# Features between two layers dealt out anew, and A12·B21 of the weight product in inner form

## The chip, the cores and the metric

The kernel runs on one core of a Trainium2 chip. The metric is the device time of one execution in microseconds; the time before is the median of three runs. Engines: TensorE (PE, with its weight loads PEld), VectorE (DVE), ScalarE (ACT), GpSimd (POOL), and SyncE (SP), which here only issues transfers.

## The reference

Two residual layers with low-rank adapters, all in float32, x of 8 × 256 × 1024:

```python
# layer 0: idx0 picks one of 5 adapters per batch row
y = x + x @ W0.T + ((x @ A0[idx0]) @ B0.T) * 0.5          # A0: (5, 1024, 32), B0: (1024, 32)
# layer 1: idx1 picks one of 32 adapters per batch row
out = y + y @ W1.T + b1 + ((y @ A1[idx1]) @ B1[idx1]) * 2  # A1: (32, 1024, 16), B1: (32, 16, 1024)
```

W0 and W1 are 1024 × 1024.

## The kernel before, in words

The kernel first multiplies the two weights, M = (I + W0)ᵀ(I + W1)ᵀ, and then applies M to all eight batch rows, together with the adapters, folded into a few narrow products. The weight product is a 2 × 2 block product in the Strassen–Winograd form: seven products of 512 × 512 blocks, called P1 = A11·B11, P2 = A12·B21 and so on, and sums of blocks on VectorE. The A blocks lie in `w0n` (W0 as loaded, with the identity added), the B blocks in `w1T` (W1 transposed, with the identity added). Later products have the same form at two levels: each product of 512 is itself seven products of 256 (`product`, with `Operand` holding the four sums t1 to t4 of the right side and `z_sums` making the four sums of the left side; `form` puts the seven results together).

The contraction index of M is the 1024 features between the layers: rows of W0 and columns of W1. Each feature stands at a partition p (0 to 127) of one of eight chunks k; chunks 0 to 3 make A11 and B11, chunks 4 to 7 make A12 and B21. Before, feature 512·i + 4·p + m stands in chunk k = 4i + m at partition p.

The stage around the change, at the start of the kernel:

- SP issues the loads in program order: the first 256 rows of the first half of W1's rows (`load_w1`, L170, four transfers, one for each group of 32 partitions), the first column halves of chunks 0 to 3 of W0 (`load_w0`, L178), the other 256 rows, the second column half of these W1 rows, chunks 4 to 7 of W0's first column half, the second half of W1's rows (eight transfers), b0, and at last the second column half of all W0 chunks. Each row piece of W1 is 128 floats, 512 bytes.
- A transfer from SP or ACT uses one of eight semaphores in turn, and waits until the previous transfer of that semaphore has landed. Transfers of ACT and SP share them.
- VectorE transposes W1 chunk by chunk (`turn_w1`, L225) and adds the identity to chunks (L233, L185); part of the identity is added on POOL.
- TensorE computes P1 in half width as the transposes arrive (L951), ACT copies the four results to `m22` (`keep_p1`, L300), and then P2 is accumulated on top of P1 in the same four banks, four tiles of 128 rows with four matmuls of 512 columns each (`product2`, L286), and copied to `m11` (L310).
- ACT issues the eight gathers of a1, the layer 1 adapter rows, one for each batch row (`load_a1`, L198), between its copies; POOL copies each into place (L202).
- Then TensorE runs `prepare_down(0)` (L701, reads a1 and the first half of w0n), `prepare_up` (L676), `finish_up` (L690), `prepare_down(1)` (L701, reads the second half), `prepare_cross` (L715), and `product6` of the first tile (L286).

The order of the instructions on each engine is the order of the program text (a manual schedule); each engine works in order. The waits are put in by the framework. It finds that an instruction reads what another has written by the range of addresses of its operand within each partition.

Of the kernel before, what the change touches and what calls it, by code (L numbers as in the profile page):

```python
# [10 lines left out]
ALU = mybir.AluOpType  # L11
# [9 lines left out]
P = 128  # L21
NH = 512
# [5 lines left out]
NWARM = 15  # L28
NV7 = 7
# [5 lines left out]
NQ = NH // 2  # L35
NB = 4
NX = 2
SQ = 32
# [4 lines left out]
def kernel(  # L43
# [11 lines left out]
    lora_b1: bass.AP,  # L55
    out: bass.AP,
):

# [70 lines left out]
    def fix_indices(rawi, n: int, layer: int):  # L131
        wrap = const.tile([1, B], I32, tag=f"wrap{layer}", name=f"wrap{layer}")
        nc.vector.tensor_scalar(wrap, rawi, 0, n, ALU.is_lt, ALU.mult)
        fixed = const.tile([1, B], I32, tag=f"fixed{layer}", name=f"fixed{layer}")
        nc.vector.tensor_tensor(fixed, rawi, wrap, ALU.add)
        nc.vector.tensor_scalar(fixed, fixed, 0, n - 1, ALU.max, ALU.min)
        return fixed

    def index(fixed, b: int, n: int, engine=SP):
        return nc.values_load(  # L140
            fixed[0:1, b : b + 1],
            engines=[engine],
            min_val=0,
            max_val=n - 1,
            skip_runtime_bounds_check_because="clamped on the chip",
        )
# [11 lines left out]
                )  # L158
        return xq

    def new_w1(h: int, i: int):
        both = units[:, 4 * h + 2 * i : 4 * h + 2 * i + 2].rearrange("p u n -> p (u n)")
        return both.rearrange("p (t c) -> p t c", t=NR)

    def load_w1(wq, h: int, i: int, lo: int = 0, hi: int = NR):

        rows = slice(h * NH + lo * SQ, h * NH + hi * SQ)
        for g in range(NG):
            cols = slice(i * NH + g * P, i * NH + (g + 1) * P)
            nc.sync.dma_start(  # L170
                wq[g * SQ : (g + 1) * SQ, lo:hi, :],
                w1[rows, cols].rearrange("(t q) c -> q t c", q=SQ),
            )

    def load_w0(k: int, i: int):
        cols = slice(i * NH, (i + 1) * NH)
        rows = w0[(k // NB) * NH : (k // NB + 1) * NH, cols]
        nc.sync.dma_start(  # L178
            w0n[:, k, cols], rows.rearrange("(p m) c -> p m c", m=NB)[:, k % NB, :]
        )  # L180

    def diag_w0(k: int):
        diag = w0n[:, k].rearrange("p (i q m) -> p i m q", i=2, m=NB)[:, k // NB, k % NB]
        engine = nc.vector if k < NB else nc.gpsimd
        engine.tensor_tensor(diag, diag, ident, ALU.add)  # L185

    def load_b0():
        nc.sync.dma_start(
            b0.rearrange("p (i m) r -> p i (m r)", i=2),
            lora_b0.rearrange("(i p m) r -> p i (m r)", i=2, m=NB),  # L190
        )


    a1_rows = work[:, 0 : 2 * NH].rearrange("p (b k r) -> p b k r", b=B, k=NK)

    def load_a1(b: int):
        j = index(fixed1, b, N1, mybir.EngineType.Activation)
        nc.scalar.dma_start(  # L198
            a1_rows[:, b].rearrange("p (i m) r -> p i (m r)", m=NB),
            lora_a1[bass.ds(j, 1)].rearrange("o (i p m) r -> p (o i) (m r)", i=2, m=NB),  # L200
        )
        nc.gpsimd.tensor_copy(a1[:, :, b, :], a1_rows[:, b])  # L202

    def load_down(b: int):
# [15 lines left out]
            )  # L220


    def turn_w1(wq, h: int, k: int, lo: int = 0, hi: int = NR):
        cols = slice(h * NH + lo * SQ, h * NH + hi * SQ)
        nc.vector.transpose(  # L225
            w1T[:, k, cols].rearrange("p (t q) -> p t q", q=SQ),
            wq[:, lo:hi].rearrange("p t (q m) -> p m t q", m=NB)[:, k % NB],
        )
        if k // NB == h:
            part = slice(lo * SQ // NB, hi * SQ // NB)  # L230
            diag = w1T[part, k, cols].rearrange("p (q m) -> p m q", m=NB)[:, k % NB]
            engine = nc.vector if h == 0 else nc.gpsimd
            engine.tensor_tensor(diag, diag, ident[part, part], ALU.add)  # L233

    def turn_x(xq, unit: int):
        xT = units[:, unit].rearrange("p (k t) -> p k t", k=NB)
# [238 lines left out]
    def quarters(x):  # L475
        return x[:, 0:2, 0:P], x[:, 2:4, 0:P], x[:, 0:2, P:T], x[:, 2:4, P:T]

    def z_sums(x, z):
        x11, x12, x21, x22 = x
        nc.vector.tensor_tensor(z[0], x21, x22, ALU.add)  # L480
        nc.vector.tensor_tensor(z[1], z[0], x11, ALU.subtract)
        nc.vector.tensor_tensor(z[2], x11, x21, ALU.subtract)
        nc.vector.tensor_tensor(z[3], x12, z[1], ALU.subtract)


    SLOT = {2: 0, 3: 1, 4: 2, 5: 3, 7: 4, 1: 5, 6: 6}
# [3 lines left out]
    def slot(ps, i: int):  # L490
        n, pos = BANK[i]
        return ps[n][:, pos * NQ : (pos + 1) * NQ]
# [78 lines left out]
    def form(v, ps=None, dst=None):  # L571
# [21 lines left out]
        nc.vector.tensor_tensor(mid, src_two(3, 0), two(1), ALU.add)  # L593
        nc.vector.tensor_tensor(d[:, 3 * NQ : 4 * NQ], src(5), at(6), ALU.add)  # L594

    m12 = {}

    def sums_m(m: int):
# [5 lines left out]
    class Chain:  # L604
# [33 lines left out]
            z_sums(self.q(name), self.z[name])  # L638

        def preload(self):  # L640

            p = m22[:, self.tiles, :].rearrange("p m (h n) -> p (m h) n", h=2)
            for i, part in ((2, 0), (4, 2), (5, 3)):
                nc.scalar.copy(slot(self.X, i), p[:, part])
            nc.vector.tensor_tensor(slot(self.X, 3), p[:, 1], p[:, 3], ALU.subtract)
            for i in (1, 7):
                nc.vector.memset(slot(self.X, i), 0.0)

        def product(self, ps, name, which, first, low=None):
            product(ps, self.q(name), self.z[name], w_ops[which], first, low=low)  # L650
# [17 lines left out]
    def prepare_up():  # L668
        tile = work[:, 4 * NH : 6 * NH]
        part = [tile[:, h * NH : (h + 1) * NH] for h in range(NO)]  # L670
        for h in range(NO):
            cols = slice(h * NH, (h + 1) * NH)
            pm = new_bank()
            for k in range(NK):
                g = k % 4
                nc.tensor.matmul(  # L676
                    pm[g * R0 : (g + 1) * R0, :],
                    b0[:, k, :],
                    w1T[:, k, cols],
                    start=(k < 4),  # L680
                    stop=(k >= NK - 4),
                )
            nc.scalar.copy(part[h], pm)
        return part
# [13 lines left out]
    def prepare_down(h: int):  # L698
        pm = new_bank()
        for k in range(NK):  # L700
            nc.tensor.matmul(  # L701
                pm,
                a1[:, k].rearrange("p b r -> p (b r)"),
                w0n[:, k, h * NH : (h + 1) * NH],
                start=(k == 0),
                stop=(k == NK - 1),
            )
        nc.scalar.copy(gT[h], pm)
# [185 lines left out]
    with tc.manual_schedule(engines=ORDERED):  # L894
        make_identity(nc, ident)
        mid = NR // 2
        wq = {}
        wq[0, 0] = new_w1(0, 0)
        for n in range(2):
            load_w1(wq[0, 0], 0, 0, n * mid, (n + 1) * mid)  # L900
            if n == 0:
                for k in range(NB):
                    load_w0(k, 0)
        wq[0, 1] = new_w1(0, 1)
        load_w1(wq[0, 1], 0, 1)
        for k in range(NB, NK):
            load_w0(k, 0)
        for i in range(2):
            wq[1, i] = new_w1(1, i)
            load_w1(wq[1, i], 1, i)  # L910
        load_b0()
        for k in range(NK):
            load_w0(k, 1)
        nc.scalar.copy(s_all[:, 0:R0], ident[:, 0:R0])

        pw = banks[6][:, 0:P]
        for _ in range(NWARM):
            nc.tensor.matmul(pw, ident, ident, start=True, stop=True)
        raw0, raw1 = load_indices(idx0, 0), load_indices(idx1, 1)
        nc.gpsimd.memset(scale, L1_SCALING)  # L920
        for half in range(2):
# [27 lines left out]
        def first(g, k: int, n: int):  # L949
            cols = slice(n * NH // 2, (n + 1) * NH // 2)  # L950
            nc.tensor.matmul(  # L951
                g.p1[:, cols],
                g.a[0][:, k, :],
                w1T[:, k, cols],
                start=False,
                stop=(k == NB - 1),
                skip_group_check=True,
            )

        for k in range(NB):  # L960
            turn_w1(wq[0, 0], 0, k, 0, mid)
            diag_w0(k)
            for g in w_groups:
                first(g, k, 0)
        for k in range(NB):
            turn_w1(wq[0, 0], 0, k, mid, NR)
        for m, g in enumerate(w_groups):
            for k in range(NB):
                first(g, k, 1)
            g.keep_p1(m22[:, m, :])  # L970
        fixed0, fixed1 = fix_indices(raw0, N0, 0), fix_indices(raw1, N1, 1)
        for k in range(NB, NK):
            turn_w1(wq[0, 1], 0, k)
        for m, g in enumerate(w_groups):
            for b in range(3 * m, min(3 * m + 3, B)):
                load_a1(b)
            g.product2(m11[:, m, :])
        for k in range(NB):
            turn_w1(wq[1, 0], 1, k)
        for k in range(NB):  # L980
            turn_w1(wq[1, 1], 1, NB + k)
        for k in range(NB, NK):
            diag_w0(k)
        for k in range(NB):
            sums_w1_first(k)
        prepare_down(0)
        part = prepare_up()
        w_groups[0].sums()
        sums_w1_last()
        finish_up(part)  # L990
        prepare_down(1)
        prepare_cross()
        for which in ("t2", "t1"):
            w_ops[which].sums_dma()
# [286 lines left out]
```

## Time and profile before

| what | value |
|---|---|
| median of 3 runs | 336.01 us (335.77 to 336.64) |
| profiled execution | 336.54 us |
| its span, first to last instruction | 334.8 us |
| granted TensorE clock, mean | 0.999 |
| PE busy | 329.6 us, 98% of the span |
| DVE busy | 246.2 us, 74% |
| POOL busy | 67.9 us, 20% |
| ACT busy | 61.3 us, 18% |
| bytes moved by DMA | 34.53 MB |

Times in the profile count from the start of the span. A matmul in float32 stands as two records, so "x32" on a matmul line is 16 matmuls. A name such as `bank<-w1T,w0n` says which tile is written and which are read; L286 is line 286 of the kernel. In a line of the timeline the numbers are the start, the time that the group took, the engine, and in brackets the idle time of the engine before it and what ended it. "SPq" and "ACTq" are the issuing of transfers on these engines, and "issue" is time in which the engine waited for nothing that the profile shows. The chain that ended last is followed back from the last instruction, each time to what released it.

### The profile page before, as it was taken

How to read it: one execution, taken by the hardware profiler on the slowest of the kernel's cores; microseconds unless marked ns; L12 is line 12 of the kernel's file. 1: busy time of each engine (PE TensorE's matmuls, PEld its weight loads, DVE VectorE, ACT ScalarE, POOL GpSimd, SP SyncE). 2: the span in 40 equal slices, each digit the busy share in tenths (PEclk: the TensorE clock that was granted, in tenths of full speed). 3: DMA queues.
4: the chain of work that ended last, by engine and by line, in shares of the span. 5: the costliest groups of instructions: out<-in, count | busy, mean ns of one | idle time of the engine just before them, and what ended most of it. 6: DMA issues, size and time to landing. Idle time of an engine off the chain costs nothing.

```text
span 334.8 us, 4443 instructions
## 1 busy us (share of the span) xinstructions
PE 329.6 (98%) x1496; PEld 245.1 (73%) x1496; DVE 246.2 (74%) x466; ACT 61.3 (18%) x128; POOL 67.9 (20%) x125
## 2 busy tenths in 40 slices
PE   8999999999999999999999999999999999999996
PEld 8774434544488877888877887877888777788875
DVE  5752697159899999999997856985675986323964
ACT  1022043300034132440001330001331001322000
POOL 7001261540042232771023100012200010000000
PEclk9999999999999999999999999999999999999999
DMA  7949982990062980786277300275500121100113
GB/s 211 199 133 186 271 191 46 168 173 14 0 95 63 194 137 14 113 133 104 95 191 204 79 2 0 74 222 148 116 10 0 63 96 63 64 2 0 63 65 126
DMA packets 66399, 34.53 MB, mean 103 GB/s; under 512 B 47300, under 2 KB 61124, under 8 KB 66376
## 3 DMA queue, kind: packets, MB, share of 16 engines
q1 hardware_dynamic: 56520, 21.13, 27.9%
q0 software_dynamic: 7680, 12.59, 17.4%
q10 hardware_dynamic: 2176, 0.52, 1.0%
q8 instruction: 12, 0.20, 0.2%
q14 instruction: 11, 0.09, 0.1%
HBM read 19.55 MB, written 8.39 MB: 83 GB/s over the span
## 4 chain that ended last, share of the span: by engine, by line
PE 94%; DMA 2%; SPq 1%; DVE 1%; issue 0%; ACT 0%; DVEq 0%
PE bank L523 66%; PE bank L286 14%; PE bank L747 4%; PE bank L701 4%; DMA units<-in_L_cond_W_dram 2%; PE bank L951 2%; PE bank L676 1%; PE bank L765 1%; SPq L170 1%; DVE w1T L225 1%; PE bank L690 1%; SPq L178 1%; DVE w1T L233 0%; PE bank L736 0%; PE bank L715 0%
## 5 line engine op out<-in xcount | busy, mean ns | idle before, releaser
L509 DVE TENSOR_TENSOR work<-bank,work 128x512 f32<-128x512 f32 (+1 forms) x56 | 32.7, 620 | 19.0 <-PE bank L523 18.8
L505 ACT COPY work<-bank 128x512 f32<-128x512 f32 (+1 forms) x56 | 25.8, 548 | 43.0 <-PE bank L523 42.6
L225 DVE STREAM_TRANSPOSE w1T<-units 128x512 f32<-128x512 f32 (+1 forms) x20 | 17.3, 901 | 18.0 <-DMA units<-in_L_cond_W_dram 17.9
L888 POOL DMA_DIRECT2D out_dram<-work x12 | 9.0, 752 | 100.6 <-DVE work L594 100.6
L523 PE MATMUL bank<-w0n,w1T 128*128 128x256 f32 x104 | 24.6, 384 | 0.0
L755 ACT ACTIVATE a<-bank,shift,scale 128x256 f32<-128x256 f32 x8 | 4.5, 564 | 103.3 <-PE bank L747 103.3
L523 PEld LDWEIGHTS bank<-w0n,w1T 128*128 128x128 f32 x104 | 19.3, 190 | 4.1 <-issue 1.7
L523 PE MATMUL bank<-w0n,m 128*128 128x256 f32 x88 | 21.2, 384 | 0.0
L523 PE MATMUL bank<-w1T,s_all 128*128 128x256 f32 x80 | 20.2, 379 | 0.0
L238 DVE STREAM_TRANSPOSE units<-units 128x512 f32<-128x512 f32 x32 | 19.9, 676 | 0.2
L523 PEld LDWEIGHTS bank<-w0n,m 128*128 128x128 f32 x88 | 16.4, 190 | 3.4 <-issue 1.4
L523 PE MATMUL bank<-tw,m 128*128 128x256 f32 x68 | 17.5, 382 | 0.0
L523 PEld LDWEIGHTS bank<-w1T,s_all 128*128 128x128 f32 x80 | 15.2, 190 | 2.1
L523 PE MATMUL bank<-tw,s_all 128*128 128x256 f32 x64 | 16.1, 379 | 0.0
L747 PE MATMUL bank<-units,down 128*64 128x256 f32 x128 | 15.6, 385 | 0.0
L523 PE MATMUL bank<-m,units 128*128 128x256 f32 x64 | 15.1, 379 | 0.0
L951 PE MATMUL bank<-w1T,w0n 128*128 128x256 f32 x64 | 14.5, 383 | 0.5 <-DVE w1T L233 0.5
L523 PEld LDWEIGHTS bank<-tw,m 128*128 128x128 f32 x68 | 12.8, 190 | 2.4 <-issue 0.7
L523 PE MATMUL bank<-w0n,s_all 128*128 128x256 f32 x56 | 14.4, 379 | 0.0
L286 PE MATMUL bank<-tw,s_all 128*128 128x512 f32 x32 | 14.3, 595 | 0.0
L951 PEld LDWEIGHTS bank<-w1T,w0n 128*128 128x128 f32 x64 | 12.3, 196 | 2.4 <-DVE w1T L233 1.3
L701 PE MATMUL bank<-w0n,a 128*128 128x512 f32 x32 | 14.1, 592 | 0.0
(249 smaller groups left out, 646.8 us busy)
## 6 DMA issues: line engine op xcount, KB each, us to landing
units<-in_x_dram SPq DMA_DIRECT2D x128, 64.0 KB, 2.4
out_dram<-work POOLq DMA_DIRECT2D x12, 512.0 KB, 3.5
w0n<-in_L_cond_W_dram SPq DMA_DIRECT2D x16, 256.0 KB, 6.1
units<-in_L_cond_W_dram SPq DMA_DIRECT2D x12, 256.0 KB, 4.9
out_dram<-work SPq DMA_DIRECT2D x3, 512.0 KB, 3.2
units<-in_L_cond_W_dram SPq DMA_DIRECT2D x8, 128.0 KB, 4.6
down<-in_L_cond_lora_A_dram SPq DMA_DIRECT2D x32, 32.0 KB, 2.4
up<-in_L_cond_lora_Bs_dram SPq DMA_DIRECT2D x16, 64.0 KB, 2.7
```

The costliest lines, as they stand in the source:

```text
L170: nc.sync.dma_start(wq[g * SQ : (g + 1) * SQ, lo:hi, :], w1[rows, cols].rearrange("(t q) c -> q t c", q=SQ),)
L225: nc.vector.transpose(w1T[:, k, cols].rearrange("p (t q) -> p t q", q=SQ), wq[:, lo:hi].rearrange("p t (q m) -> p m t q", m=NB)[:, k % NB],)
L238: nc.vector.transpose(xT[:, NX * j : NX * (j + 1), :].rearrange("p c (t q) -> p c t q", q=SQ), xq[:, :, j, :].rearrange("p t (q c) -> p c ...
L286: nc.tensor.matmul(pm, a[:, k, :], b(k), start=first and k == 0, stop=(k == NB - 1), skip_group_check=not first,)
L505: nc.scalar.copy(at_home(v, n), whole(ps, n))
L509: nc.vector.tensor_tensor(at_home(v, n), whole(ps, n), at_home(v, n), ALU.add)
L523: nc.tensor.matmul(slot(ps, i) if dst is None else dst, lhs, rhs, start=BANK[i][0] not in started, stop=stop, skip_group_check=True,)
L701: nc.tensor.matmul(pm, a1[:, k].rearrange("p b r -> p (b r)"), w0n[:, k, h * NH : (h + 1) * NH], start=(k == 0), stop=(k == NK - 1),)
L747: nc.tensor.matmul(pl[half * MLOW : (half + 1) * MLOW, :], down[:, half * NB + k, :], x_b[half][:, k, :], start=(k == 0), stop=(k == NB - ...
L755: nc.scalar.activation(lows[:, b % NLOW], pl, mybir.ActivationFunctionType.Identity, bias=shift[:, 0:1], scale=scale[:, 0:1],)
L888: eng.dma_start(out[b, :, h * NH : (h + 1) * NH].rearrange("(j p) d -> p j d", p=P), ob[:, 0:D].rearrange("p (j d) -> p j d", d=NH),)
L951: nc.tensor.matmul(g.p1[:, cols], g.a[0][:, k, :], w1T[:, k, cols], start=False, stop=(k == NB - 1), skip_group_check=True,)
```

## The change

Feature 256·g + 128·i + 4·q + m now stands in chunk k = 4i + m at partition 32·g + q. So a group of 32 partitions holds 256 neighbouring columns of W1, both halves i, and one transfer of the second half of W1's rows reads row pieces of 256 floats, 1024 bytes. The first half of the rows is still loaded in pieces of 128 floats (`first`, `last`). W0, b0 and a1 are loaded in the same new order; b0 takes two transfers, and each a1 gather becomes two, the first half on ACT and the second on POOL. The diagonal on which the identity stands now lies apart for each group of partitions: `add_identity` does four chunks in one instruction, `add_identity_to` one chunk; all of them run on VectorE.

P2 = A12·B21 is computed in the inner form, for two tiles of 128 rows at a time (class `Second`): seven products of 256 columns with 256 features each, two matmuls a product, on banks that are loaded with parts of P1 beforehand (`load_inner`, `load_inner_3`, `zero_inner`), so that `form` gives P1 + P2 in `m11`. `prepare_down(1)` moves from behind `finish_up` to behind the identities, ahead of `prepare_up`, and the loads of W0's second column half move behind the identities of chunks 4 to 7 in the program. The warm-up matmuls write to four banks instead of one.

```diff
-    def load_w1(wq, h: int, i: int, lo: int = 0, hi: int = NR):
+    def load_w1(h: int, lo: int, hi: int, first: int = 0, last: int = 2):

         rows = slice(h * NH + lo * SQ, h * NH + hi * SQ)
         for g in range(NG):
-            cols = slice(i * NH + g * P, i * NH + (g + 1) * P)
+            cols = slice((2 * g + first) * P, (2 * g + last) * P)
             nc.sync.dma_start(
-                wq[g * SQ : (g + 1) * SQ, lo:hi, :],
+                wq[h][g * SQ : (g + 1) * SQ, lo:hi, first * P : last * P],
                 w1[rows, cols].rearrange("(t q) c -> q t c", q=SQ),
             )
...
+    def add_identity(t, i: int, first: int, last: int):
+
+        part = slice(first * SQ, last * SQ)
+        corner = t[part, NB * i, (2 * first + i) * P : (2 * first + i) * P + 1]
...
+        nc.vector.tensor_tensor(diag, diag, one, ALU.add)
...
     def load_a1(b: int):
-        j = index(fixed1, b, N1, mybir.EngineType.Activation)
-        nc.scalar.dma_start(
-            a1_rows[:, b].rearrange("p (i m) r -> p i (m r)", m=NB),
-            lora_a1[bass.ds(j, 1)].rearrange("o (i p m) r -> p (o i) (m r)", i=2, m=NB),
-        )
+        for i, engine in enumerate((nc.scalar, nc.gpsimd)):
+            j = index(fixed1, b, N1, engine.engine)
+            rows = lora_a1[bass.ds(j, 1)].rearrange("o (g i q m) r -> i g (o q) (m r)", g=NG, i=2, m=NB)
+            engine.dma_start(
+                a1_rows[:, b, NB * i : NB * (i + 1)].rearrange("p m r -> p (m r)"),
+                rows[i],
+            )
         nc.gpsimd.tensor_copy(a1[:, :, b, :], a1_rows[:, b])
...
+    class Second:
...
+        def __init__(self, n: int):
+            self.tiles = slice(2 * n, 2 * n + 2)
+            self.ps = sets[1 - n]
+            a = w0n.rearrange("p k (j q c) -> p j k c q", j=NK // NX, c=NX)[:, n, NB:NK]
+            self.x = a[:, 0:2, 0], a[:, 2:4, 0], a[:, 0:2, 1], a[:, 2:4, 1]
+            z = s_all[:, (2 + n) * D : (3 + n) * D].rearrange("p (i c t) -> p i c t", i=4, c=2)
+            self.z = [z[:, i] for i in range(4)]
...
+        def products(self, plan):
+            product(self.ps, self.x, self.z, self.op, "loaded", plan=plan)
...
         for m, g in enumerate(w_groups):
             for k in range(NB):
                 first(g, k, 1)
             g.keep_p1(m22[:, m, :])
-        fixed0, fixed1 = fix_indices(raw0, N0, 0), fix_indices(raw1, N1, 1)
+            if m % 2:
+                load_inner(seconds[m // 2].ps, seconds[m // 2].tiles)
+                for b in range(4 * (m // 2), 4 * (m // 2) + 4):
+                    load_a1(b)
+        one, other = seconds
         for k in range(NB, NK):
-            turn_w1(wq[0, 1], 0, k)
-        for m, g in enumerate(w_groups):
-            for b in range(3 * m, min(3 * m + 3, B)):
-                load_a1(b)
-            g.product2(m11[:, m, :])
-        for k in range(NB):
-            turn_w1(wq[1, 0], 1, k)
-        for k in range(NB):
-            turn_w1(wq[1, 1], 1, NB + k)
-        for k in range(NB, NK):
-            diag_w0(k)
+            turn_w1(0, k)
+        add_identity(w1T, 1, 0, 2)
+        add_identity(w0n, 1, 0, 2)
+        for k in range(NK):
+            load_w0(k, 1)
+        zero_inner(other.ps)
+        one.products([1, 2])
+        other.products([1, 2])
+        z_sums(one.x, one.z, 0, 2)
+        Second.op.sums()
+        z_sums(one.x, one.z, 2, 4)
+        load_inner_3(one.ps, one.tiles)
+        one.products([6, 5, 4, 7, 3])
+        keep(one.kept, one.ps)
+        load_inner_3(other.ps, other.tiles)
+        z_sums(other.x, other.z)
+        other.products([6, 5, 4, 7, 3])
+        keep(other.kept, other.ps)
+        prepare_down(0)
+        for n in range(2):
+            for k in range(NK):
+                turn_w1(1, k, n * mid, (n + 1) * mid)
+        for i in range(2):
+            add_identity(w1T, i, 2, 4)
+        for k in range(NK):
+            add_identity_to(w0n, k, 2, 4)
+        prepare_down(1)
+        part = prepare_up()
         for k in range(NB):
             sums_w1_first(k)
-        prepare_down(0)
-        part = prepare_up()
         w_groups[0].sums()
+        for second in seconds:
+            second.form()
         sums_w1_last()
         finish_up(part)
-        prepare_down(1)
         prepare_cross()
```

## The prediction

> **What bounds the kernel now.** I read the page first, for who is busy and when.
>
> ```profile
> span 334.8 us, 4443 instructions
> ...
> PE 329.6 (98%) x1496; PEld 245.1 (73%) x1496; DVE 246.2 (74%) x466; ACT 61.3 (18%) x128; POOL 67.9 (20%) x125
> ...
> GB/s 211 199 133 186 271 191 46 168 173 14 0 95 63 194 137 14 113 133 104 95 191 204 79 2 0 74 222 148 116 10 0 63 96 63 64 2 0 63 65 126
> ```
>
> TensorE (PE) is busy 98% of the span. A change inside the first 60 us counts in full if it moves the moment from which TensorE runs without a gap. The chain that ended last, in order of time, gives that stage (start, us, what):
>
> ```profile
> 16.43 5.89 PE bank L951 x26
> 22.32 13.73 PE bank L286 x32
> 36.05 6.87 PE bank L701 x16
> 42.92 3.57 PE bank L676 x32
> 46.49 1.91 PE bank L690 x4
> 48.41 6.87 PE bank L701 x16
> 55.27 0.57 PE bank L715 x16
> 55.85 3.63 PE bank L286 x8
> ...
> 91.96 27.63 PE bank L523 x128
> ```
>
> A11·B11 ends at 22.32, A12·B21 (L286, two records a matmul) takes 13.73, then come the adapter products (L701 prepare_down, L676 prepare_up, L690, L715), and at 55.85 the first product6. From 36.05 to 55.85 are 19.80 us that the change keeps, in another order. The reader should see no gap: whatever arrives late after 22 shifts all that follows. Then the transfers, in the timeline, the DMA view and the source view of the a1 loads:
>
> ```profile
> 24.94 0.29 POOL L202 COPY a<-work 128x128 f32<-128x128 f32 x1 [16.29 <-DMA work<-in_L_cond_lora_As_dram]
> 33.89 1.01 POOL L202 COPY a<-work 128x128 f32<-128x128 f32 x3 [1.36 <-DMA work<-in_L_cond_lora_As_dram]
> 38.59 0.33 SPq L178 DMA_DIRECT2D w0n<-in_L_cond_W_dram  x1
> ```
>
> ```profile
> w0n<-in_L_cond_W_dram SPq DMA_DIRECT2D x16, 256.0 KB, 6.1
> work<-in_L_cond_lora_As_dram ACTq DMA_DIRECT2D x8, 64.0 KB, 4.9
> idx<-in_itok_B_dram POOLq DMA_DIRECT2D x2, 0.0 KB, 3.5
> ```
>
> ```profile
> DMA to landing us min/median/max: 1.9/4.9/5.5
> ```
>
> The eight a1 copies end at 34.9, just before L701 needs them; the second column half of w0n is issued at 34.30 to 39.4 (the line at 38.59 is its k = 6) and lands 6.1 us after issue; the small POOL load takes 3.5.
>
> **The change, part by part.**
>
> *TensorE's own work.* Removed: 16 matmuls of 512 columns, 13.73 us. Added: 28 of 256 columns (two groups of seven products, two matmuls each) at 27.63/64 = 0.432, 12.09 us. Alone, −1.64.
>
> *The first sum waits for loads it does not read.* The eight second-half loads of w0n now stand in the program ahead of the first z_sums. In the program as it is built, VectorE's first z_sums instruction carries waits for the second halves of k = 4 and k = 6: its operand steps over two rows of w0n, and the range from its first to its last element covers them. Before, nothing on VectorE that A12·B21 needs waits for these loads. VectorE works in order, so behind that sum stand the operand sums (t2 first needed), the other z_sums, all 16 transposes of W1's second half, the identities, sums_w1_first. TensorE can do products 1 and 2 of both groups (8 matmuls, 3.5 us, by about 29) and then waits for z[1] and t2.
> When does k = 6 land? Before: 38.59 + 6.1 = 44.7. The load queue keeps its brakes: SP's W1 loads wait in turn for a1 loads on ACT, and ACT issues those a bit earlier now (three bank copies of 0.38, then issues about 0.95 apart from 20.6; the second four after 26.5), but one more W1 load stands behind them. I take 44.7. Lower end: W1's 2 MB at the 271 GB/s of the page's fifth slice (mostly w0n's 2048-byte rows) instead of 199 in the second (512-byte rows) is 10.5 − 7.7 = 2.8 less, 41.9. Upper end: one more 256 KB ahead at 199 GB/s and the a1 waits, 46.7.
> From 44.7: two sums of 256 columns 0.80 (L480 to L482 start to start), two operand sums of 512 columns 1.40 (L599 to L601), so t2 at 46.9. TensorE: 20 remaining matmuls, 8.63, to 55.6. VectorE meanwhile needs another 1.2 (t1, t4), 0.67, 0.86 (load_inner_3 twice) and 1.47, which is ahead of TensorE's use.
>
> *The restart.* TensorE will have idled from 29 to 47. How it runs after idling shows in the busy windows of TensorE alone:
>
> ```profile
> 1.40:4.00 2.60, 2.60 (x12) 1.00 0.67 163
> 7.40:10.00 2.60, 2.60 (x14) 1.00 1.18 233
> ```
>
> The first has 128-column records of the warm-up, the second 256-column ones: the same rate of records for half the columns, though the granted clock reads 1.00 in both. The warm-up's 30 records take 6.11 us. So a start from idle costs up to half of some 5.2 us, 2.6. Ends: 0 and 2.6; I take 2.6, as this gap (18 us) is longer than the idle 1.4 us of the start. The products end at 58.2.
> [...]
>
> *a1 half on POOL.* load_a1 is now, for each b, one 32 KB load on ACT, one on POOL, then POOL's copy, which waits for both. POOL works in order (in the waits view its second kind of accumulating issue waited 2.0 us for a landing with the next issue behind it), so load b+1 on POOL starts after copy b: eight round trips, where before ACT issued ahead. One step: index and registers 0.5 (ACT's issue spacing 0.95 less its 0.44 issue), issue to landing 3.5 (the idx row, nearest: small and on POOL), copy 0.3, signals 0.05: 4.35. Ends: 2.9 (landing 2.0, the least of SP's 32 KB loads of down) and 6.35 (landing 5.5, the loaded end of the a1 row). The first copy ends near 23.3 (ACT's first a1 load issues at 20.9, lands 1.9 later), the last 7 steps on: 53.8, ends 43.6 and 67.8. prepare_down(0) reads all eight, so TensorE cannot start it before. At 53.8 it is hidden under 58.2; from a step of 5.0 it is the bound.
>
> *The rest.* Identities leave POOL (L185 3.85 us, L233 four times 0.52) for ten small VectorE adds, about 3.2; transposes of half width cost 16 × 0.64 instead of 8 × 1.02, +2.1; form on both groups, 2 × 2.6. VectorE from 44.7: 6.4 of sums to 51.1, transposes to 61.4, identities to 64.7, sums_w1_first to 70.0, group 0's sums to 72.5, forms to 77.7. prepare_down(1) needs the identities at 64.7 and starts at 65.1; product6 needs 71.3 and starts at 78: covered, by 0.4 and 6.7. If that cover went, prepare_down(1) would be late. One more b0 issue on SP, 0.44, is within the end of 46.7. The A11·B11 stage keeps its loads and sizes: 0.
>
> *Sum.* 58.2 + 19.80 = 78.0 for the first product6 instead of 55.85: +22.2, and 0.3 (0 to 0.9) because VectorE's sums_w1_last and sums for t4 now end at 82.7, just behind product6. The profiled execution took 336.54, 1.74 beside its span, and lies 0.53 over the median 336.01; the shift goes on the median: 358.5.
>
> *1024-byte rows.* By the slices their gain is at most the 2.8 us above, in a transfer; it is inside the lower end of 41.9.
> [...]
>
> **Rivals.**
> A, POOL's chain is last: steps of 5.0 to 6.35, center 5.6: copies end at 62.5, product6 at 82.3, 362.8; top 368. For it: the ACT loads of the same table took 4.9 under W1's traffic, which fills most of this stretch. Against: half the bytes.
> B, loads early and no slow restart: k = 6 at 41.9, products end at 52.8, POOL's 53.8 binds: product6 at 73.6, 354. For it: 271 GB/s; against: SP's waits for a1, which bandwidth does not shorten.
> C, the other side: nothing waits anew, and the shorter product shows. Place: 22.3 to 36.05. Price: −1.64, +0.9 for the two identities ahead of it (2 × 0.42 after the last transpose at 22.4), 335.3. It decides only if the first sum can run by 25 and a POOL step is at most (36 − 23.3)/7 = 1.8. No row is near either: 44.7, and 2.9 at the least.
>
> **How the numbers follow.** Forecast 0.60 (own range 355 to 361, from the ends of landing and restart), A 0.25, B 0.10, C 0.05. The range 352.5 to 366 takes in B and A but for its top; it leaves out C and some 0.07 of A. 0.3% (1 us) is about what a measurement here can tell from no change; C alone gives faster (0.03) or same (0.02); all else is slower, 0.95.
>
> **What would show it.** Right: VectorE idle for some 17 us before the first z_sums, released by the load of w0n; TensorE idle from about 29 to 47 behind VectorE; POOL copies of a1 4 to 5 us apart; the first product6 near 78; later stages as long as before. Wrong: z_sums running near 25, a1 copies closer than 3 us, or TensorE stopped in later stages. If TensorE's gap ends at POOL's last a1 copy instead, A holds.

## The result, and the profile after

The changed kernel takes 389.86 us (median of four runs, 388.87 to 389.89) against 336.32 us before (the median of four runs; the three ahead of the prediction gave 336.01): 1.158 times as long, 95% interval 1.156 to 1.161. The forecast was 358.5, with a range up to 366.

The page of the changed kernel, the lines that answer to those of before:

```profile
span 388.2 us, 4595 instructions
...
PE 336.6 (87%) x1520; PEld 253.5 (65%) x1520; DVE 260.3 (67%) x514; ACT 64.2 (17%) x138; POOL 68.4 (18%) x125
...
PEclk9887855579999999999999999999999999999999
...
GB/s 107 143 113 88 183 103 99 101 1 110 26 95 204 0 0 84 120 178 42 94 131 88 120 213 142 15 1 80 213 150 49 0 54 95 76 23 0 54 56 108
```

The span is 53.4 longer. Nearly all of it lies ahead of the first product6: from there to the end the kernel takes 279.4, before 279.0 (product6 starts at 108.77 and at 55.78 in the timelines). The loss is in the first eleven slices of 9.7 us. While the weights come in, the slices now move 88 to 143 GB/s (one of them 183), where before they moved 133 to 271, and three slices in a row stand at 103, 99 and 101. The granted clock falls to 0.5 in slices 6 to 8.

The chain that ended last, in order of time (start, us, what), from the a1 loads to the adapter products:

```profile
42.68 7.95 DMA work<-in_L_cond_lora_As_dram
50.65 0.56 SPq L205
...
55.30 3.14 SPq L180
...
58.48 2.82 SPq L180
...
61.35 14.24 DMA w0n<-in_L_cond_W_dram
...
77.98 11.07 PE bank L541 x40
89.05 13.73 PE bank L754 x32
```

Before, this part of the chain was TensorE alone. Now it goes from a gather of a1 on ACT to SP's queue, through issues of chunks 4 and 5 that take about 3 us where before one took 0.3 to 0.5, to the load of chunk 6, issued at 61.35 and landed 14.2 later. And the timeline, first VectorE, then TensorE:

```profile
37.95 0.60 DVE L193 TENSOR_TENSOR w0n<-w0n,ident 64x256 f32<-64x256 f32 x1 [6.66 <-DMA w0n<-in_L_cond_W_dram]
...
75.71 0.42 DVE L501 TENSOR_TENSOR s_all<-w0n 128x256 f32<-128x256 f32 x1 [36.56 <-DMA w0n<-in_L_cond_W_dram]
```

```profile
25.51 5.89 PE L1005 MATMUL bank<-w1T,w0n 128*128 128x256 f32 x26 [0.20 <-DVE w1T L201]
38.65 5.07 PE L541 MATMUL bank<-w1T,w0n 128*128 128x256 f32 x16 [7.26 <-issue]
77.98 3.78 PE L541 MATMUL bank<-s_all 128*128 128x256 f32 x8 [34.26 <-DVE s_all L437]
...
88.89 13.90 PE L754 MATMUL bank<-w0n,a 128*128 128x512 f32 x32
...
108.77 3.70 PE L300 MATMUL bank<-tw,s_all 128*128 128x512 f32 x8
```

The forecast's mechanism is at work: VectorE's first sum waits 36.56 for a load that it does not read, TensorE behind it 34.26. But P1 (L1005) ends at 31.4 instead of 22.3, the loads behind it are late as well, and the first product6 comes at 108.77, not 78.0.

### The profile page after: what moved, and what is told of

The parts are those of the page before. It is cut to its first block, busy times and chain, and to the rows that moved or that the text cites. A ratio compares the mean times of both kernels' runs of the same rounds, so it can differ in the third digit from the quotient of the medians.

```text
span 388.2 us, 4595 instructions
## 1 busy us (share of the span) xinstructions
PE 336.6 (87%) x1520; PEld 253.5 (65%) x1520; DVE 260.3 (67%) x514; ACT 64.2 (17%) x138; POOL 68.4 (18%) x125
## 4 chain that ended last, share of the span: by engine, by line
PE 78%; DMA 8%; SPq 5%; ACTq 3%; ACT 2%; DVE 2%; issue 1%; DVEq 0%
PE bank L541 60%; PE bank L300 8%; PE bank L800 4%; DMA w0n<-in_L_cond_W_dram 4%; PE bank L754 4%; SPq L180 3%; DMA units<-in_L_cond_W_dram 3%; DMA work<-in_L_cond_lora_As_dram 2%; ACTq L217 2%; SPq L172 2%; PE bank L729 1%; PE bank L818 1%; ACTq L141 1%; ACT units L445 1%; DVE w1T L244 1%
## 5 line engine op out<-in xcount | busy, mean ns | idle before, releaser
L541 PE MATMUL bank<-s_all 128*128 128x256 f32 x24 | 7.7, 471 | 34.3 <-DVE s_all L437 34.3
L541 PEld LDWEIGHTS bank<-s_all 128*128 128x128 f32 x24 | 5.6, 237 | 35.6 <-DVE s_all L437 34.7
L501 DVE TENSOR_TENSOR s_all<-w0n 128x256 f32<-128x256 f32 x4 | 1.8, 443 | 36.6 <-DMA w0n<-in_L_cond_W_dram 36.6
L1005 PE MATMUL bank<-w1T,w0n 128*128 128x256 f32 x64 | 18.6, 449 | 4.9 <-DMA w0n<-in_L_cond_W_dram 2.4
L541 PE MATMUL bank<-w1T,s_all 128*128 128x256 f32 x88 | 22.3, 379 | 0.0
L244 DVE STREAM_TRANSPOSE w1T<-units 128x256 f32<-128x256 f32 (+1 forms) x28 | 17.6, 688 | 3.7 <-DMA units<-in_L_cond_W_dram 3.6
L1005 PEld LDWEIGHTS bank<-w1T,w0n 128*128 128x128 f32 x64 | 13.6, 224 | 9.7 <-issue 3.5
L541 PEld LDWEIGHTS bank<-w1T,s_all 128*128 128x128 f32 x88 | 16.7, 190 | 2.3
```

The lines of the kernel that those rows point to most:

```text
L244: nc.vector.transpose(w1T[:, k, cols].rearrange("p (t q) -> p t q", q=SQ), wq[h][:, lo:hi].rearrange("p t (i q m) -> p i m t q", i=2, m=NB ...
L541: nc.tensor.matmul(slot(ps, i) if dst is None else dst, lhs, rhs, start=BANK[i][0] not in started, stop=stop, skip_group_check=True,)
L1005: nc.tensor.matmul(g.p1[:, cols], g.a[0][:, k, :], w1T[:, k, cols], start=False, stop=(k == NB - 1), skip_group_check=True,)
```

## The experiments

Two theories stood at first. P: the new W0 loads are slow in themselves, because their outermost step is now the group of 32 partitions, so a transfer of 128 partitions is described as 4 × 32 rows where it was 128 rows. F: the loads are late because of what they wait for. Later a third was added, that three causes hide one another: P, the first sum's wait (S), and the arrangement of the a1 loads (A).

### Is it the pattern? The kernel before, with other outermost steps

In the kernel before only W0's loads are altered; nothing else, no size, order or wait. The run with 4 groups has the changed kernel's `load_w0`; the others have 16, 8 and 2 in place of NG.

```diff
     def load_w0(k: int, i: int):
         cols = slice(i * NH, (i + 1) * NH)
-        rows = w0[(k // NB) * NH : (k // NB + 1) * NH, cols]
-        nc.sync.dma_start(
-            w0n[:, k, cols], rows.rearrange("(p m) c -> p m c", m=NB)[:, k % NB, :]
-        )
+        rows = w0.rearrange("(g i q m) c -> i m g q c", g=NG, i=2, m=NB)[k // NB, k % NB]
+        nc.sync.dma_start(w0n[:, k, cols], rows[:, :, cols])
```

> The kernel before with W0's loads alone taken from the changed kernel (outermost step of 4). The rows of W0 then stand on other partitions than the features of W1, so the product is of other pairs and the output is not the reference's; every instruction, size and wait is that of the kernel before. Theory P: the A11 B11 stage, whose matmuls wait for the first four loads, ends 6 to 12 late, at 28 to 34, and the time is 343 to 355. Rival F (the pattern costs nothing): 335 to 338, the stage ends at 22.3.

> As the run with the pattern in the kernel before, but with an outermost step of 16 groups of 8 partitions instead of 4 groups of 32: rows equally scattered, the same 128 runs of 2048 bytes a load. The rows stand on other partitions than W1's features want, so the output is not the reference's. Theory P (a load moves at some 99 GB/s with an outermost step of 4, as the 2.6 us between landings of 256 KB show, because its outermost step sets how much of the transfer runs side by side): with 16 there is nothing left of the 24 us, 335 to 339. Rival R (the scattered rows, or the extra dimension, cost the time): 355 to 362, as with 4.

> The same with an outermost step of 8 groups of 16 partitions, other rows again. Theory P: some 198 GB/s a load, close to the 171 to 211 that the slices of the kernel before show while W0 and W1 come in: 336 to 344. Rival R: 355 to 362.

> The same with an outermost step of 2 groups of 64 partitions, other rows again. Theory P: half of 99 GB/s, so 5.2 us for each 256 KB; sixteen loads take 84 us where they took 42 with 4 groups: 336 + 24 + 42, 390 to 412. Rival R: 355 to 362.

| outermost step of W0's loads | us | against 336 to 337 before |
|---|---|---|
| 16 groups of 8 | 336.89 | 0 |
| 8 groups of 16 | 342.96 | +6 |
| 4 groups of 32 (the change) | 360.21 | +23 |
| 2 groups of 64 | 400.97 | +64 |

Three of the four lie in the window of theory P; with 4 groups the price was larger than expected (343 to 355). Each is a single execution. Rows just as scattered, with the same added dimension, cost nothing with 16 groups, so F and the scattered rows are out for this part. The page's rate in 40 slices of 10 us, of the run with 2 groups:

```profile
GB/s 73 60 120 84 66 129 107 95 50 50 61 93 141 140 69 15 72 178 145 32 104 143 86 165 187 66 2 53 163 179 81 2 53 80 53 53 2 34 73 106
```

Where W0's second column half comes alone (the ninth and tenth slices), 50 GB/s move. In the changed kernel, with 4 groups, this window of 25 us (start and end, length, busy times of the engines, clock, share of the DMA engines, GB/s) holds the same loads and some a1:

```profile
51.00:76.00 25.00, 0.00 (x0) 0.00 (x0) 0.29 (x1) 0.00 (x0) 4.48 (x9) 0.50 0.32 103
```

So some 25 GB/s for each group: 50 with two, 99 to 103 with four. With 8 groups the busiest slices among the weight loads have 166 to 192, near what the kernel before reaches with everything, so what 8 groups alone allow is not seen there. The busy share of the 16 DMA engines says the same. From 80 to 90 us with 2 groups it is 0.13, at 50 GB/s; from 57 to 63 us with 4 groups in the kernel before, where W0's second column half also comes alone, it is 0.26, at 98 GB/s. Of 16 engines that is as much as about 2 and 4 busy throughout. The queue shows it too. SP's timeline in the kernel before, and then the same kernel with 4 groups:

```profile
4.60 6.09 SPq L170 DMA_DIRECT2D units<-in_L_cond_W_dram  x8
```

```profile
2.67 2.50 SPq L178 DMA_DIRECT2D w0n<-in_L_cond_W_dram  x4
5.21 14.65 SPq L170 DMA_DIRECT2D units<-in_L_cond_W_dram  x8
```

Eight loads of W1, whose own pattern is unchanged, took 14.65 to issue behind four such loads; in the kernel before they took 6.09.

Here one side of the transfer has 128 partitions and the other 16, 8, 4 or 2 groups. With 4 and 2 groups the busy shares above are close to 4/16 and 2/16, and the cost in time grows as the groups get fewer: 0, 6, 23 and 64 us. Which engines carried the bytes, and by what the outermost step sets the rate, no view shows.

### Each cause undone alone in the changed kernel

P undone: one W0 load takes 32 partitions and four chunks.

```diff
-    def load_w0(k: int, i: int):
-        cols = slice(i * NH, (i + 1) * NH)
-        rows = w0.rearrange("(g i q m) c -> i m g q c", g=NG, i=2, m=NB)[k // NB, k % NB]
-        nc.sync.dma_start(w0n[:, k, cols], rows[:, :, cols])
+    def load_w0(g: int, i: int, half: int):
+        cols = slice(half * NH, (half + 1) * NH)
+        rows = w0.rearrange("(g i q m) c -> g i q m c", g=NG, i=2, m=NB)[g, i]
+        nc.sync.dma_start(
+            w0n[g * SQ : (g + 1) * SQ, NB * i : NB * (i + 1), cols], rows[:, :, cols]
+        )
```

> The changed kernel with W0 loaded by groups of 32 partitions (one load takes 32 partitions, four rows of 2048 bytes each, 256 KB; sixteen loads as before, on the same queue at the same places), instead of 128 partitions whose outermost step is the group of 32, 4 of them. Nothing else differs; the a1 and b0 loads keep their outermost step of 4. Theory P (the pattern with an outermost step of 4 makes W0's loads slow): the A11 B11 stage ends near 22 again instead of 31.4, the second half of W0 lands near 45, and the forecast's own figures come true for the rest: the first product6 between 76 and 84, the time 357 to 366. Rival F (the loads are late because of what they wait for, the order in the queue and the a1 issues on ScalarE, not because of their pattern): 383 to 391, w0n loads still over 0.5 us an issue and the A11 B11 stage over 29.

Measured 380.21, in neither window. P1 ended at 27.0, nearer to before. But SP then stood still:

```profile
5.51 6.66 SPq L172 DMA_DIRECT2D units<-in_L_cond_W_dram  x8
13.83 18.37 SPq L180 DMA_DIRECT2D w0n<-in_L_cond_W_dram  x4
32.46 13.37 SPq L172 DMA_DIRECT2D units<-in_L_cond_W_dram  x8
```

Four loads of W0 took 18.37: in the program as it is built they take turns on semaphores that ACT's a1 loads use, and ACT issues these only from 24.95, behind its copies of P1. One of the four waited 12.3 for an a1 load alone. The second half of W0 landed near 65 and TensorE waited 27.18 for it, already in products 1 and 2, since a load now covers four chunks, and among what it writes is what they read. With the first wait gone, the next one binds.

S undone: the second-half loads of W0 move behind the sums.

```diff
-        for k in range(NK):
-            load_w0(k, 1)
         zero_inner(other.ps)
...
         z_sums(other.x, other.z)
+        for k in range(NK):
+            load_w0(k, 1)
         other.products([6, 5, 4, 7, 3])
```

> The changed kernel with the second-half loads of W0 moved in program order behind the last z_sums, so that no z_sums waits for a load it does not read (and the loads wait for the sums). The 4-group pattern stays. Theory P plus the first sum's wait as the forecast has it: the first half of rows 4 to 7 still lands only near 38, the sums run at 40 to 46 instead of 75.7, the products end near 55 to 60, the first product6 comes at 75 to 90 and the time is 355 to 371. If the first sum's wait were not what holds the products (another wait is just behind): 380 to 391.

Measured 385.41, a miss by 14, and in the window of the rival (another wait just behind). The sums ran at 38.4 to 44.6 and the products ended at 52.8, both a little ahead of what was expected, but then TensorE waited for a1:

```profile
51.80 1.03 PE L541 MATMUL bank<-w1T,s_all 128*128 128x256 f32 x4
81.28 17.05 PE L754 MATMUL bank<-w0n,a 128*128 128x512 f32 x32 [28.45 <-POOL a L221]
```

This is the forecast's rival A, hidden in the changed kernel behind the sum's wait: the a1 copies on POOL came 3 to 9 us apart, the last at 80.43.

A undone: all sixteen a1 loads on POOL, one after the other ahead of the eight copies, none on ACT.

```diff
-        for i, engine in enumerate((nc.scalar, nc.gpsimd)):
-            j = index(fixed1, b, N1, engine.engine)
+        j = index(fixed1, b, N1, mybir.EngineType.Pool)
+        for i in range(2):
...
-            engine.dma_start(
+            nc.gpsimd.dma_start(
...
-                for b in range(4 * (m // 2), 4 * (m // 2) + 4):
-                    load_a1(b)
+                for b in range(B):
+                    (copy_a1 if m // 2 else load_a1)(b)
```

> The changed kernel with the a1 loads alone altered: all sixteen on GpSimd's queue, issued one after the other ahead of the eight copies, none on ScalarE. The loads of SP then share no semaphore with ScalarE's late a1 loads, and no a1 load stands behind a copy. The 4-group pattern of W0 and the first sum's wait stay. Theory (three causes, each hiding behind another): SP's W1 and second-half W0 loads go out up to 15 earlier, the second half of W0 lands near 60 instead of 75.7, the time is 365 to 382. If the a1 arrangement held nothing but itself (its last copy at 79.3 lay 10 under prepare_down in the changed kernel): 387 to 391.

Measured 389.35, in the rival's window. The 0.5 is less than a single execution can tell, as the changed kernel's own four runs are 1.0 apart. SP's W1 loads went out 11 us earlier (27.4 instead of 38.7), a1 was complete by 43.9, but W0's second half started only 1.2 earlier and landed at 75.2 instead of 75.7. So with the pattern in place the landing follows the slow transfers, and not the semaphores that SP waits for.

### Two and three causes undone

The pairs use the same edits, but in the table S means from here on that the second-half loads go behind all fourteen products; in the run above they went behind the sums. With P undone this is needed, since a load over four chunks covers what TensorE's products read. Times without an interval are single executions, beside 336 to 337 of the kernel before.

> Both edits: W0 by groups of 32 partitions, and the second-half loads behind the sums. The a1 loads stay as changed, half on GpSimd, one behind the other. Theory P and the wait of the first sum, both as the forecast has them: nothing holds the products, they run from 22 to about 36, and the a1 chain on GpSimd is next: its last copy between 53 and 70 sets prepare_down, so the first product6 at 73 to 90, 353 to 370. If the a1 chain is faster than that (steps under 3 us): 336 to 346. If P is wrong: as e3, over 355 with the A11 B11 stage over 29.

> The changed kernel with W0 by groups of 32 partitions and its second-half loads behind all the products of both groups; a1 as changed (half on ScalarE, half on GpSimd, one behind the other). Theory: SP's W0 loads wait for the semaphores of ScalarE's a1 loads as in the other runs that keep them (the last first-half load of W0 issued at 31), so the products start near 36 and end near 50, and prepare_down waits for the last a1 copy at 65 to 71: first product6 at 85 to 91, 368 to 374. If without the new wait the a1 chain is quicker too: 355 to 367.

> a1 ahead on GpSimd and W0 by groups of 32 partitions, the second-half loads in their place, so the false wait of the sums stays (TensorE's first products wait for them too, since a load now spans four rows). This is the forecast's own case without its a1 chain: theory: the second half of W0 lands near 44 and the first product6 comes at 74 to 80, the time 351 to 361. Rival (the false wait is worth nothing once the loads are quick): 336 to 346.

> a1 ahead on GpSimd and the second-half loads of W0 in program order behind all fourteen products of both groups, the 4-group pattern staying. Theory: the products end near 53 as in the run with the loads behind the sums, a1 is long there, and the adapter products wait for the slow second half of W0: first product6 at 72 to 88, time 349 to 366. Rival (the pattern costs only the first stage): product6 at 66 to 70, 345 to 348.

> All three: W0 by groups of 32 partitions, second-half loads behind all the products, a1 ahead on GpSimd. Theory: nothing of the three is left; the products of A12 B21 run from the end of the A11 B11 stage (22 to 27) without a gap, the first product6 comes at 54 to 62, the time is 334 to 342. If a fourth cause is behind them (GpSimd's queue, the identities on VectorE, the clock): over 345, and the wait is read from TensorE's rows.

| undone | us |
|---|---|
| nothing (the changed kernel) | 389.86 |
| A | 389.35 |
| S (loads behind the sums) | 385.41 |
| P | 380.21 |
| S and A | 376.29 |
| P and S | 374.77 (372.20 with the loads ahead of the second group's products) |
| P and A | 367.82 |
| P, S and A | 347.85, 1.035 of before (1.033 to 1.037) |

With P and S undone, prepare_down waited 19.23 for the last a1 copy (374.77); both runs of this pair came out 1 to 2 above their windows. Undone alone, A, S and P give 0.5, 4.5 and 9.7; undone together they give 42.0. Put back alone into the last row, A costs 26.9, P 28.4 and S 20.0. So each is hidden by the others. P and A undone is the forecast's own case without its a1 chain; it missed its window (351 to 361) by 7:

```profile
53.23 5.11 PE L545 MATMUL bank<-w1T,w0n 128*128 128x256 f32 x14 [24.88 <-DMA w0n<-in_L_cond_W_dram]
...
86.69 3.70 PE L304 MATMUL bank<-tw,s_all 128*128 128x512 f32 x8
```

From the landing to the first product6 are 33.5; the forecast had 78.0 − 44.7 = 33.3, the changed kernel shows 108.77 − 75.71 = 33.1. That 33.5 is so near is partly luck, since here TensorE also had seven of the eight matmuls of products 1 and 2 left, which ran while VectorE made its sums. The miss is the landing, 53.2 where I expected 44. The loads start at 33.29, no later than before (34.30), but SP took 11.83 to issue the eight where it had taken 5.10. b0 and a1 still had 4 groups here. In the three runs below that load b0 too by 32 partitions the eight took 8.0 to 8.1, so b0's pattern can be a part of it; the rest stays open.

The run with S and A undone missed its window by 10. VectorE's identities follow the landings of W0's second half, 2.6 to 2.9 apart:

```profile
68.99 0.27 DVE L201 TENSOR_TENSOR w0n<-w0n,ident 64x64 f32<-64x64 f32 x1 [2.38 <-DMA w0n<-in_L_cond_W_dram]
71.63 0.27 DVE L201 TENSOR_TENSOR w0n<-w0n,ident 64x64 f32<-64x64 f32 x1 [2.38 <-DMA w0n<-in_L_cond_W_dram]
74.54 0.27 DVE L201 TENSOR_TENSOR w0n<-w0n,ident 64x64 f32<-64x64 f32 x1 [2.63 <-DMA w0n<-in_L_cond_W_dram]
```

Its first product6, at 87.63, still lay in the expected 72 to 88. The rest of the miss is behind it: TensorE waited 4.71 for ACT's copy of `cross` (L786), and the product after that wait took 6.09 instead of 3.60.

### What stays with all three undone

347.85 missed its window (334 to 342) and lies in that of a fourth cause (over 345). P1 ended 5.1 late, as the first matmul needs four whole loads now and starts at 11.72 instead of 7.33. TensorE waited 1.94 and 0.64 in prepare_down, behind identities for which W0 came late, and 2.65 behind the first product6. Four more runs divide this.

One: a1 of the first token alone (two loads, copied eight times).

> The run with all three edits, but a1 loaded for the first token alone (two loads instead of sixteen, copied eight times; the output is not the reference's for the other seven). It measures what the sixteen a1 loads, still with an outermost step of 4, cost the loads beside them. Theory: W1's second half, which landed 15 to 16 after issue, lands 6 to 8 after; the waits of the adapter products for W0 (1.94 and 0.64) go, and the time falls from 347.9 to 341 to 345. Rival: the a1 loads are too small to matter (1 MB in 34): 347 to 349.

342.50, in the theory's window: the a1 loads cost 5.4. (They are 0.5 MB, not the 1 MB of the expectation, in pieces of 256 bytes.)

Two: every load by 32 partitions, a1 and b0 too, the first W0 loads in halves.

```diff
+        rows = lora_a1[bass.ds(j, 1)].rearrange("o (g i q m) r -> g q (o i) (m r)", g=NG, i=2, m=NB)
+        for g in range(NG):
+            nc.gpsimd.dma_start(
+                a1_rows[g * SQ : (g + 1) * SQ, b].rearrange("p (i m) r -> p i (m r)", i=2),
+                rows[g],
+            )
```

> The run with all three edits, and the pattern taken out of the last places: a1 by 32 partitions (32 loads of 16 KB on GpSimd, ahead of the copies), b0 by 32 partitions, and the first four W0 loads in halves of two rows (eight of 128 KB), so that the first identity waits for half as much. Theory: a1's transfers stop slowing W1 (worth up to 5.4, as the run with one a1 showed), the first matmul starts 1 to 2 earlier than 11.7; the longer row of a1 issues on GpSimd (32 at 0.5 to 0.7, from 14.5 to about 36) gives back up to 3: 336 to 344. Rival (the rest is the inner form itself, its sums and identities): 345 to 349.

352.90 (1.050 of before, 1.047 to 1.053) is worse, and for a reason that neither the theory nor the rival named. P1 and the products were in time, and TensorE waited for a1, whose 32 small loads on one queue, with the copies, took until 50:

```profile
24.67 3.70 PE L545 MATMUL bank<-w1T,w0n 128*128 128x256 f32 x16 [2.01 <-DMA w0n<-in_L_cond_W_dram]
...
50.55 15.69 PE L758 MATMUL bank<-w0n,a 128*128 128x512 f32 x32 [13.54 <-POOL a L225]
```

Three: that run with a1 in sixteen loads again, issued ahead of the first transposes.

> The run with all loads by 32 partitions, but a1 again in sixteen loads of 128 partitions on GpSimd, and the fixing of the indices and these loads moved ahead of the first transposes, so that GpSimd issues them from about 9 instead of 14.5. Theory: a1 is copied by 35 to 38, the adapter products follow the products at 37 to 40, first product6 at 57 to 61, 337 to 342; the early a1 loads share their four lanes with the first stage's W1 and W0, which may cost the first stage 1 to 3. Rival (a1 anywhere in this stretch costs what it did): 346 to 350.

345.75 (1.029, 1.025 to 1.032) is just under the rival's window. a1 was out of the way, but TensorE waited 6.76 for W0 ahead of the products, where it waited 2.01 in the run before this one: with a1 loaded early, W0 came late. That a1's loads keep to four engines ("four lanes") is an estimate from the busy share of 0.26 of 16 that W0's loads with 4 groups had; for a1 alone no view shows it.

Four: the second run, with a1 of the first token alone (four loads).

> The run with all loads by 32 partitions, with a1 loaded for the first token alone (four loads of 16 KB, copied eight times; the output is not the reference's for the other seven). Nothing of a1 is left in the way. Theory (the inner form saves its 1.4 on TensorE and pays it back in the wait for the second half of W0's first half and in the late sums): first product6 at 55 to 59, 334.5 to 339. Rival (VectorE's extra identities and half transposes bind): 341 or more, with TensorE waiting for VectorE ahead of product6.

341.19 is above the theory's window and in the rival's, though the wait is not where the rival put it. TensorE's timeline in the kernel before, then in this run, then ACT's:

```profile
55.78 3.70 PE L286 MATMUL bank<-tw,s_all 128*128 128x512 f32 x8
...
60.89 3.60 PE L286 MATMUL bank<-tw,s_all 128*128 128x512 f32 x8
```

```profile
23.93 3.70 PE L545 MATMUL bank<-w1T,w0n 128*128 128x256 f32 x16 [1.53 <-ACT bank L647]
...
36.10 13.90 PE L758 MATMUL bank<-w0n,a 128*128 128x512 f32 x32
...
55.98 3.70 PE L304 MATMUL bank<-tw,s_all 128*128 128x512 f32 x8
...
62.70 0.74 PE L793 MATMUL bank<-ident,work 128*128 128x128 f32 x4 [2.32 <-ACT cross L788]
63.28 5.29 PE L304 MATMUL bank<-tw,s_all 128*128 128x512 f32 x8
```

```profile
60.56 1.67 ACT L449 ACTIVATE units<-w1T 128x512 f32<-128x512 f32 x3 [2.12 <-DVE w1T L383]
62.14 0.51 ACT L788 COPY cross<-bank 32x128 f32<-32x128 f32 x2
```

The first product6 is at 55.98, before at 55.78. The fourteen products take 12.17 instead of 13.7, and 1.53 of waiting for ACT's copies into the banks ahead of them give the gain back. Behind it VectorE is late with `sums_w1_last` (L383), ACT waits 2.12 for it with its copy of `cross` queued behind, and TensorE waits 2.32 for that copy. Its next product then takes 5.29 instead of 3.60: the granted clock is 0.50 from 63.3 to 66.3. The 2.32 and these 1.7 make up the 3.9 by which the rest of the span is longer; 0.5 more lies around the span.

Two things stand ahead of `sums_w1_last` on VectorE that the kernel before did not have there, and no run parts them: a wait of 3.69 for the last loads of W0's second half (ahead of its identities at 45.63), and the two forms, 4.9. Each is longer than the 2.12 that ACT waited. So 341.19 need not be the price of the inner form alone; a wait for a load is still in it. No version came under the kernel before.

## Why the prediction was wrong

The sign, the chain of waits and most terms were right. The step that failed is "When does k = 6 land? … I take 44.7". It landed at 75.6: 30.9 of the 31.4 between 358.5 and 389.86. I took the issue at 38.59 and the 6.1 to landing from the kernel before, with ends of 41.9 and 46.7, although the diff gives these very loads another outermost step. In the changed kernel chunk 6 was issued at 61.35 (22.8 later) and landed 14.2 after (8.1 more). For the same reason "The A11·B11 stage keeps its loads and sizes: 0" failed, a term put at nothing: the stage ended at 31.4 instead of 22.3, as W0's loads for it landed late.

What the runs put in its place: loads with 4 groups move at 98 to 103 GB/s, and they alone made the kernel before 23 slower. With P undone the landing came near 65, with P and A undone at 53.2. The last 8.5 go with SP's slow issues of these loads (11.83 instead of 5.10), whose cause stays open in part. I had counted the loads and their bytes, and never asked whether one load of the same bytes still costs the same. The forecast's sentence on the queue's brakes (SP waits for a1 loads) saw the coupling but priced it as before. It cost more: SP's W1 loads waited 19.8 in all for a1 loads (9.4 before), and ACT's a1 issues started at 29.29, not 20.6, and came 1.7 apart instead of 0.95.

Point by point, the rest:

- *First sum*: right. VectorE idled behind a load of w0n, and TensorE behind VectorE. Undoing it alone gives just 4.5 because the a1 chain stood right behind; the forecast had named that chain as rival A.
- *Sums and products after the landing, restart*: 13.5 forecast (44.7 to 58.2), 13.2 measured (75.71 to 88.89). The 20 matmuls took 10.9, so the restart cost 2.3 where 2.6 was taken. This time the granted clock shows it: TensorE idled from 43.7, the clock read 1.00 until 48.3, then 0.50 until 82.4, 4.4 after the first matmul behind the gap, and then 1.00.
- *a1 on POOL*: forecast 4.35 a step, 53.8 at the end; measured 6.0 a step (37.14 to 78.98), within its ends, and 79.3 at the end, since the first copy ended 14.1 late and each step took 1.6 more. It was covered by the even later sums, by 9.6; the run with the loads behind the sums showed it as the bound.
- *The adapter products*: 19.80 forecast, 19.88 measured. *Behind the first product6*: 0.3 forecast, 0.4 measured. VectorE's other work was covered in the changed kernel, as said.
- *1024-byte rows*: no run isolates them. Only the loads of the second half of W1's rows have them; P1 reads the first half, in pieces of 512 bytes as before, so its end (22.4 in the last run, 22.3 before) says nothing of them.
- *Rival C*, nothing waits anew, 335.3: the last run comes nearest to it, and its TensorE term (−1.64; measured 12.17 against 13.7) was right, but 341.19 shows two waits beside it: 1.53 ahead of the products, for which there was no term, and 3.9 behind product6 with the slow product, where 0.3 (0 to 0.9) was taken.
- The range held its ends for the landing from rows of the old pattern alone. A bound for an altered transfer has to come from a row with that pattern; there was none in the trace, and the text did not say so.

## What to carry to other kernels

When a diff regroups the dimensions of a transfer, price it as a new transfer, even with the same bytes and rows: here the outermost step set the rate, some 25 GB/s for each group with two and with four groups. When one wait hides another, undoing one tells little; the price of each is seen by putting it back into a version without any. And a load that stood behind slow ones in the queue (14.65 us to issue eight that took 6.09), or waited for the semaphore of a late one (12.3 for one a1 load), was late too here, so count what stands behind it.

## What the runs showed of the hardware that I had not expected

- The same 128 row pieces of 2048 bytes moved at 50 GB/s with an outermost step of 2 and at 98 to 103 with 4; with 16 the kernel was as fast as with 128 (336.89 against 336 to 337).
- Behind the slow transfers the issue of the next ones was long: in the changed kernel six of the eight issues of unchanged W1 loads on SP took 1.2 to 4.0 us behind loads with 4 groups, where they took 0.4 to 1.1 before. What stood behind them on SP waited: the next four W0 loads were issued from 23.24, before from 11.62.
- Behind 2.32 us in which TensorE idled came a slow stretch: the next product took 5.29 instead of 3.60, at a granted clock of 0.50 (last run). In the run with all three undone a gap of 2.65 at the same place was followed by 3.60, at a granted clock of 1.00. What makes the difference stays open.
